# Attention's output projection: all heads in one tile of 128 rows, and three jobs placed later behind POOL

## The chip, the cores and the metric

The kernel runs on one core of a Trainium2 chip. The metric is device time of one execution in microseconds. Before the change it is 6233.53 us, the median of 3 runs (6230.06 to 6236.76).

## The reference, cut to what matters

Two layers run one after the other on `x` of shape (4, 128, 64, 64), float32, that is 4 images of 4096 tokens with 128 channels.

```python
# layer 0: attention over the tokens of one image, 4 heads of 32 channels
Q, K, V = split_heads(x_flat @ Wq + bq), ...
attn = softmax(einsum('bhnd,bhmd->bhnm', Q, K) * scale)
out  = einsum('bhnm,bhmd->bhnd', attn, V)          # heads side by side: 128 channels
y    = out @ Wo + bo + x_flat                      # output projection and residual
y    = layernorm(y) * gamma + beta                 # over the 128 channels of a token
# layer 1: three branches of y, summed
spatial  = conv3x3(y) + bias
spectral = irfft2(W_spec applied to rfft2(y))
ym       = mamba(y)       # in_proj, 4-tap conv, silu, selective scan of 256 x 16 states, gate, out_proj
```

## The kernel before, in words

**Chunks, halves, slots and steps.** The tokens are cut into 32 chunks of 512. A chunk's four heads are handled as two halves `H` (two heads each, `k = H % 2`), and a half meets the image's 4096 keys in 32 tiles of 128. One such tile is a step, and 64 steps, one chunk's two halves, are a slot. The outermost loop counts steps `t` and writes the order of all engines by hand; no scheduler changes it. A slot's number here is that of the chunk whose attention runs in it, and a step's number runs from 0 to 63 within its slot.

**What every step does.** PE computes the scores of one tile for the exponentials (`scores_for_exp`, L480: four matmuls of Q and K and two that subtract the maxima `MX`), the scores for the next half's maxima (`scores_for_max`, L436: four matmuls) and the previous tile's product with the values (`times_values`, L500: two matmuls into `po`). ACT takes the exponentials `e` (L488). DVE reduces the second scores to maxima `part` (L443). Each of these scores has one PSUM buffer, so PE cannot write the next before ACT or DVE has read the last. On even steps DVE also runs one state of layer 1's scan (L817), two slots behind; ACT makes its decay `dA` (L801) and POOL its input term `db` (L806, two states ahead), its product with C (`hs`, L827) and its sum (`acc`, L846).

**Everything else is a job.** A job is a Python generator that `Plan.step` moves on. At each `yield` it names what it needs: a place on PE (`P`), DVE (`D`) or ACT (`A`) and a PSUM bank (`B`, two in all, `m0` and `m1`). During attention an odd step has two places on each engine, an even one has one on ACT. An empty `yield` only waits for the next step. Instructions on POOL and loads on SP's queue need no place. `plan.at(t, rank, job)` starts a job at a step.

**The jobs around the change.** The last step of a half evicts `po`, which has 33 rows for each of two heads, 32 of values and one of the softmax's sum, at rows 0 and 64: ACT copies the first (L509) and DVE the second (L510) into `oz[k]`, one fixed tile for each half of a chunk whose unused rows stay zero. `normalise` then takes the two sum rows through DRAM (`zd`, `zc`), inverts them on DVE (L524), spreads the inverse over the rows by DMA (`rd`, then `rz`, L530) and multiplies on POOL (L533). `output_projection` adds the folded bias `bo` to the residual `xr` on ACT (L548) and, for each of four tiles of 128 tokens, accumulates two matmuls of `oz` with a zero-padded `Wo` (L556) and one of `xr` with the identity (L557) in `py`. `bn_stats` (L564), a reciprocal root on ACT and POOL, and `xh` (L587) follow; `xh` releases layer 1's input jobs: transposes `pt` (L638), input projections (L664), four-tap convolution on DVE (L674, L679), sigmoids in steps on ACT, DVE (L611) and POOL, projections `pd` (L700) and `pdt` (L714). The DT job ends in three POOL multiplies for each half of the 256 channels (`spe`, `dt`, `u`: L739 to L741) and a scaling of `xs` on ACT that waits for them (L748). `maxima` gathers a half's maxima on DVE (`mx`, L449), widens them on POOL (`wide`, L452), transposes them on PE (`pm`, L459) and forms `MX` on ACT and DVE (L466, L467), which the half's first scores need. `scan_output` gates a chunk's scan sums on POOL (L938) and projects them on PE (L948). `convolve` is nine matmuls (L891) and one more. `project_q` (L412) and `project_kv` (L350, L364) make Q, K and V.

**Start and tail.** All constants are loaded by DMAs that ACT issues (L197 to L251) ahead of its first activation, `khi` (L355). After the last half the scan of the last two chunks goes on alone, with its input term on DVE and its sum on PE (L839, L840).

Of the kernel before, what the change touches and what calls it, by code (L numbers as in the profile page):

```python
# [9 lines left out]
F32 = mybir.dt.float32  # L10
F32R = mybir.dt.float32r
AF = mybir.ActivationFunctionType
ALU = mybir.AluOpType
# [4 lines left out]
P = 128  # L18
W = 64
HEADS = 4  # L20
HD = P // HEADS
PAIRS = HEADS // 2
HS = P // 2
L = 512
RPC = L // W
TPC = L // P
# [129 lines left out]
def attention_then_conv_mamba(  # L156
# [17 lines left out]
    nc = tc.nc  # L174
# [3 lines left out]
    NT = N // P  # L178
# [4 lines left out]
    const = ctx.enter_context(tc.tile_pool(name="const", bufs=1))  # L183
    att = ctx.enter_context(tc.tile_pool(name="att", bufs=2))
# [10 lines left out]
    for h in range(HEADS):  # L195
        k, j = divmod(h, 2)
        nc.scalar.dma_start(wk_t[:, h, :], wk[k, :, j * HS : j * HS + HD])  # L197
    wat = const.tile([P, 1 + PAIRS, P], F32, name="wat_vo")
    nc.scalar.dma_start(wat[:, 0, :], wvo[0])
    for h in range(HEADS):  # L200
        k, j = divmod(h, 2)
        c = COL["bk"] + k
# [2 lines left out]
        )  # L205
    Wk = wk_t.rearrange("c h d -> c (h d)")
    Wv = wat[:, 0, :]
    Wo = [wat[:, 1 + k, :] for k in range(PAIRS)]

    wq_t = const.tile([P, PAIRS, 2, 2, HD], F32, name="wq_t")  # L210
    bq = const.tile([P, PAIRS], F32, name="bq")
    for h in range(HEADS):
        k, j = divmod(h, 2)
        c = COL["bq"] + h
# [10 lines left out]
    nc.scalar.dma_start(cst, consts[:, :K_SEL])  # L225
    sel_f = loc.tile([P, P], F32, tag="sg0", name="sel_f", bufs=1)
    nc.scalar.dma_start(sel_f, consts[:, K_SEL:])
    bvk = const.tile([P, PAIRS], F32, name="bvk")
    nc.vector.memset(wat[:, 1:, :], 0.0)
    nc.vector.memset(bvk, 0.0)  # L230
    for h in range(HEADS):
        row = h % 2 * HS
        hs = slice(h * HD, (h + 1) * HD)
        nc.scalar.dma_start(wat[row : row + HD, 1 + h // 2, :], wvo[1, hs, :])
        nc.scalar.dma_start(
            bvk[row : row + HD, h // 2 : h // 2 + 1], bv[0:1, hs].rearrange("o c -> c o")
        )
    vec = const.tile([P, NCOL], F32, name="vec")
    nc.scalar.dma_start(vec, vecs)
    cw = const.tile([P, 9, P], F32, name="cw")  # L240
# [16 lines left out]
    ident = cst[:, K_ID : K_ID + P]  # L257
# [13 lines left out]
    bo = const.tile([P, 1], F32, name="bo")  # L271
# [6 lines left out]
    def constants_of_the_rest():  # L278


        yield ""
        half = loc.tile([P, 2, 2 * P], F32, tag="sg1", name="half", bufs=1)
        nc.vector.tensor_scalar(half, spw, 0.5, None, ALU.mult)
        rr, ir = half[:, 0, :P], half[:, 0, P:]
        ri, ii = half[:, 1, :P], half[:, 1, P:]
        yield ""
        g_id = loc.tile([P, P], F32, tag="ob", name="g_id", bufs=1)
        nc.gpsimd.tensor_tensor(g_id, rr, ii, ALU.add)
        nc.gpsimd.tensor_tensor(cw[:, 4, :], cw[:, 4, :], g_id, ALU.add)
        nc.gpsimd.tensor_tensor(g_flip, rr, ii, ALU.subtract)  # L290
        nc.gpsimd.tensor_tensor(g_hil, ri, ir, ALU.subtract)
        nc.gpsimd.tensor_tensor(g_fliphil, ri, ir, ALU.add)
        yield ""
        nc.vector.tensor_scalar(sbias, cst[:, K_G : K_G + W], col("spec_bi"), None, ALU.mult)
        nc.vector.tensor_tensor(sbias[:, 0:1], sbias[:, 0:1], col("spec_br"), ALU.add)

        nc.scalar.activation(negA, vec[:, COL["A_log"] : COL["A_log"] + NH * NS], AF.Exp)
        yield ""
        nc.vector.tensor_scalar(negA, negA, -1.0, None, ALU.mult)


        bank = yield "PB"
        pb = bank_tile(bank, [P, 1], "pb")
        for k in range(PAIRS):
            nc.tensor.matmul(pb, Wo[k], bvk[:, k : k + 1], start=k == 0, stop=k == PAIRS - 1)
        yield "D"
        plan.release(bank, 2)
        nc.vector.tensor_tensor(bo, pb, col("bo"), ALU.add)
# [5 lines left out]
        [const.tile([P, L], F32R, name=f"K_{k}_{i}") for i in range(NCH)] for k in range(PAIRS)  # L314
    ]
    VA = [const.tile([P, TPC, HEADS, HD + 1], F32, name=f"V_{i}") for i in range(NCH)]

    oz = [const.tile([P, L], F32, name=f"oz{k}") for k in range(PAIRS)]
    for k in range(PAIRS):
        nc.gpsimd.memset(oz[k], 0.0)  # L320
    state = const.tile([P, NH * NS], F32, name="state")
    carry = const.tile([P, NH, TAPS - 1], F32, name="carry")

    rows = [slice(j * HS, (j + 1) * HS) for j in range(2)]
    used = [slice(j * HS, j * HS + HD + 1) for j in range(2)]

    plan = Plan(2, {"x": 2, "f": 1})

    def bank_tile(bank, shape, name):
        return psum.tile(shape, F32, tag=f"m{bank}", name=name)  # L330
# [114 lines left out]
    def maxima(H):  # L445

        bank = yield "B"
        mx = att.tile([P, TPC, 2], F32, tag="mx", name=f"mx_{H}")
        nc.vector.tensor_reduce(mx, part.pop(H), AX.X, ALU.max)  # L449
        wide = att.tile([P, TPC, 2, HS], F32, tag="wide", name=f"wide_{H}", bufs=1)  # L450
        for t in range(TPC):
            nc.gpsimd.tensor_copy(  # L452
                wide[:, t], mx[:, t].unsqueeze(2).to_broadcast([P, 2, HS])
            )
        yield ""
        yield ""
        pm = bank_tile(bank, [P, L], f"pm_{H}")
        for t in range(TPC):
            nc.tensor.transpose(  # L459
                pm[:, t * P : (t + 1) * P], wide[:, t].rearrange("p j d -> p (j d)"), ident  # L460
            )
        yield ""
        plan.release(bank, 2)
        mhi = att.tile([P, L], F32R, tag="th", name=f"mhi_{H}", bufs=1)
        mm = att.tile([P, L], F32R, tag="MX", name=f"MX_{H}")
        nc.scalar.activation(mhi, pm, AF.Copy, scale=-1.0)  # L466
        nc.vector.scalar_tensor_tensor(mm, mhi, minus_lo, pm, ALU.mult, ALU.subtract)  # L467
        MX[H] = mm

    es, po = {}, {}  # L470

    def scores_for_exp(H, m):

# [17 lines left out]
    def times_values(H, m):  # L491

        k = H % PAIRS
        i, t = divmod(m, TPC)
        assert have["V", i] == H // PAIRS // NCH
        if m == 0:
            po[H] = psum.tile([P, L], F32, tag="o", name=f"po_{H}")
        e = es.pop((H, m))
        for j in range(2):
            nc.tensor.matmul(  # L500
                po[H][used[j], :],
                VA[i][:, t, 2 * k + j, :],
                e[:, j, :],
                start=m == 0,
                stop=m == NT - 1,
            )
        if m == NT - 1:
            p = po.pop(H)
            nc.scalar.activation(oz[k][used[0], :], p[used[0], :], AF.Identity)  # L509
            nc.vector.tensor_copy(oz[k][used[1], :], p[used[1], :])  # L510

    def normalise(H, t0):

        k = H % PAIRS
        yield ""
        zd = dram.tile([2, L], F32, tag="zd", name=f"zd_{H}")
        for j in range(2):
            nc.sync.dma_start(zd[j : j + 1, :], oz[k][j * HS + HD : j * HS + HD + 1, :])
        yield ""
        zc = att.tile([P, 2 * L // P], F32, tag="zc", name=f"zc_{H}")  # L520
        nc.sync.dma_start(zc, zd.rearrange("h (a c) -> (h a) c", c=2 * L // P))
        yield ""
        yield ""
        nc.vector.reciprocal(zc, zc)  # L524
        rd = dram.tile([2, L], F32, tag="rd", name=f"rd_{H}")
        nc.sync.dma_start(rd.rearrange("h (a c) -> (h a) c", c=2 * L // P), zc)
        yield ""
        r = att.tile([P, L], F32, tag="r", name=f"rz_{H}", bufs=1)
        for j in range(2):
            nc.sync.dma_start(r[rows[j], :], rd[j : j + 1, :].to_broadcast([HS, L]))  # L530
        yield ""
        yield ""
        nc.gpsimd.tensor_tensor(oz[k], oz[k], r, ALU.mult)  # L533
        if k == PAIRS - 1:
            plan.at(t0, 0, output_projection(H // PAIRS))

    xrs = {}

# [4 lines left out]
    def output_projection(c):  # L543


        xr = xrs.pop(c)
        yield "A"
        nc.scalar.activation(xr, xr, AF.Identity, bias=bo)  # L548
        bank = yield "PB"
        py = bank_tile(bank, [P, TPC, P], f"py_{c}")  # L550
        for t in range(TPC):
            if t == TPC // 2:
                yield "P"
            ts = slice(t * P, (t + 1) * P)
            for k in range(PAIRS):
                nc.tensor.matmul(py[:, t, :], oz[k][:, ts], Wo[k], start=k == 0, stop=False)  # L556
            nc.tensor.matmul(py[:, t, :], xr[:, ts], ident, start=False, stop=True)  # L557


        yield "D"  # L560
# [7 lines left out]
        r = att.tile([P, TPC], F32, tag="rs", name=f"r_{c}")  # L568
# [355 lines left out]
    def scan_output(c):  # L924
# [13 lines left out]
                nc.gpsimd.tensor_tensor(accs[c, hf], accs[c, hf], gates[c][hf], ALU.mult)  # L938
        if not late:
            wr = load_flipped(c)  # L940
        yield ""
        yield ""
        bank = yield "PB"
        pf = bank_tile(bank, [P, L], f"py1_{c}")
        for hf in range(NH):
# [43 lines left out]
    for b in range(B):  # L989


        t0 = (b * NCH - 1) * SLOT + 5
# [7 lines left out]
    for H in range(HALVES):  # L1000
        if H % PAIRS == 0:
            plan.at((H - 1) * NT - LEAD - 24, 0, load_q(H // PAIRS))
        plan.at((H - 1) * NT - LEAD - 14, 0, project_q(H))
        plan.at(H * NT - LEAD, 0, maxima(H))
        plan.at((H + 1) * NT + 1, 0, normalise(H, (H + 1) * NT + 9))
    for c in range(CHUNKS):
        t0 = (c + 1) * SLOT
        plan.at(t0, 0, load_residual(c))
# [127 lines left out]
```

## Time and profile before

| | |
|---|---|
| median of 3 runs | 6233.53 us (6230.06 to 6236.76) |
| the profiled execution | 6236.14 us, of which the program's span is 6234.4 |
| mean granted TensorE clock | 0.982 |
| busy share of the span | PE 96%, POOL 73%, DVE 69%, ACT 58% |
| output projection, L556 and L557 | 768 matmul records, 2 for each matmul |
| transposes of maxima, L459 | 256 records, 1 for each |
| POOL's multiplies L533 | 64, mean 1280 ns |
| idle PE in 2483.62 to 2667.26 us | 0.68 us of 183.64 |
| idle PE in 5063.60 to 5250.66 us | 4.54 us of 187.06 |

The span is that of the one execution that the profiler recorded. Busy shares are averages over the whole span; a stretch has to be read from the timeline, which gives start, duration and, in brackets, how long the engine was idle before and what ended it. A matmul's end is modelled, so the distance between starts tells more than the duration. A float32 matmul leaves two records, a transpose one. Lines that write a tile of the program are named by it, without its number.

### The profile page before, as it was taken

To read this page: it belongs to the slowest core of one execution; us is meant where nothing else is said; L and a number is where in the kernel's file an instruction comes from. 1 tells how busy PE (TensorE), PEld (TensorE's weight loads), DVE (VectorE), ACT (ScalarE), POOL (GpSimd) and SP (SyncE) were. 2 spreads that over 40 slices of the span, in tenths; PEclk is the share of its full clock that TensorE was granted. 3 is DMA by queue.
4 is the path that set the end of the run, shared out by engine and by line. 5 is a ranking of instruction groups with operands and counts; after the bars stand their busy time and mean duration, and the time that the engine had idled before them with its cause. 6 is when DMAs were issued, how large, how long until landed. Compare 5 with 4: busy or idle time off the path is not lost. (4 is left out here: it accounts for less than half of the span.)

```text
span 6234.4 us, 83338 instructions
## 1 busy us (share of the span) xinstructions
PE 6005.2 (96%) x32076; PEld 2540.9 (41%) x32076; DVE 4286.5 (69%) x4406; ACT 3585.0 (58%) x4858; POOL 4579.0 (73%) x4819
## 2 busy tenths in 40 slices
PE   5999999999999999999999999999999999999966
PEld 2444444444444444444444444444444444444321
DVE  4556776777777676777667777776777666767647
ACT  1455666565666555666656566665566556556643
POOL 0005887778887777888787888777788777778877
PEclk7999999999999999999999999999999999999987
DMA  3001222223222222222322221122322211112223
GB/s 111 14 25 47 63 56 61 63 64 98 79 71 60 63 65 60 62 63 73 89 82 65 61 65 60 57 64 67 98 66 71 55 54 54 54 55 58 63 80 85
DMA packets 234624, 404.97 MB, mean 65 GB/s; under 512 B 39272, under 2 KB 40816, under 8 KB 234224
## 3 DMA queue, kind: packets, MB, share of 16 engines
q1 hardware_dynamic: 229840, 397.75, 22.6%
q8 instruction: 251, 4.11, 0.3%
q10 hardware_dynamic: 4384, 1.89, 0.1%
q14 instruction: 149, 1.22, 0.1%
HBM read 350.54 MB, written 49.02 MB: 64 GB/s over the span
## 5 line engine op out<-in xcount | busy, mean ns | idle before, releaser
L443 DVE TENSOR_REDUCE part<-s 128x2 f32<-128x1024 f32 x2048 | 2501.7, 1222 | 1627.4 <-PE s L436 1625.9
L488 ACT ACTIVATE e<-s 128x1024 f32<-128x1024 f32 x2048 | 2095.5, 1023 | 2271.7 <-PE s L480 2263.0
L500 PE MATMUL po<-e,V 128*33 128x512 f32 x8192 | 2160.9, 606 | 2.6 <-DVE oz L510 0.3
L480 PE MATMUL s<-Q,K 64*128 64x512 f32 x8192 | 1504.7, 445 | 22.3 <-ACT e L488 18.5
L436 PE MATMUL s<-K,Q 64*128 64x512 f32 x8192 | 1322.2, 400 | 41.2 <-DVE part L443 39.6
L827 POOL TENSOR_TENSOR hs<-hs,bc 128x512 f32<-128x512 f32 x952 | 1215.5, 1277 | 177.5 <-DVE hs L817 108.6
L480 PEld LDWEIGHTS s<-Q,K 64*128 64x128 f32 x8192 | 610.7, 185 | 1748.9 <-ACT e L488 1179.0
L806 POOL TENSOR_TENSOR db<-u,bc 128x512 f32<-128x512 f32 x948 | 1214.8, 1281 | 0.0
L846 POOL TENSOR_TENSOR acc<-acc,hs 128x512 f32<-128x512 f32 x900 | 1150.9, 1279 | 70.5
L817 DVE TENSOR_TENSOR_SCAN hs<-dA,state,db 128x512 f32<-128x512 f32 x832 | 1060.7, 1275 | 86.0 <-ACT dA L801 54.0
L436 PEld LDWEIGHTS s<-K,Q 64*128 64x128 f32 x8192 | 766.3, 186 | 276.7 <-DVE part L443 99.4
L480 PE MATMUL s<-MX,sel 64*128 64x512 f32 x4096 | 810.9, 392 | 0.0
L826 POOL COPY state<-hs 128x1 f32<-128x1 f32 x864 | 160.2, 185 | 844.8 <-DVE hs L817 844.8
L801 ACT ACTIVATE dA<-dt,negA 128x512 f32<-128x512 f32 x1024 | 702.6, 686 | 116.0 <-DVE hs L817 63.6
L500 PEld LDWEIGHTS po<-e,V 128*33 128x33 f32 x8192 | 299.3, 109 | 913.8 <-issue 879.7
L480 PEld LDWEIGHTS s<-MX,sel 64*128 64x128 f32 x4096 | 384.6, 185 | 92.6
L891 PE MATMUL pf<-xp,cw 128*128 128x512 f32 x576 | 288.2, 617 | 0.0
L452 POOL COPY wide<-mx 128x128 f32<-128x128 f32 x256 | 63.4, 294 | 200.7 <-DVE mx L449 200.7
L817 DVE TENSOR_TENSOR_SCAN hs<-dA,zero,db 128x512 f32<-128x512 f32 x128 | 163.2, 1275 | 7.7 <-POOL db L806 7.4
L840 PE MATMUL acc<-V,cst 128*128 128x512 f32 x128 | 90.1, 807 | 78.2 <-POOL V L827 78.0
L533 POOL TENSOR_TENSOR oz<-oz,rz 128x512 f32<-128x512 f32 x64 | 81.9, 1280 | 107.1 <-DMA rz<-rd 107.1
L891 PEld LDWEIGHTS pf<-xp,cw 128*128 128x128 f32 x576 | 96.2, 188 | 132.4 <-issue 127.4
(144 smaller groups left out, 3847.8 us busy)
## 6 DMA issues: line engine op xcount, KB each, us to landing
bc<-bcd SPq DMA_DIRECT2D x487, 512.0 KB
K<-kd SPq DMA_DIRECT2D x64, 256.0 KB
rz<-rd SPq DMA_DIRECT2D x128, 128.0 KB
K<-bcd SPq DMA_DIRECT2D x42, 256.0 KB
vd<-vst SPq DMA_DIRECT2D x32, 264.0 KB
V<-vd SPq DMA_DIRECT2D x32, 264.0 KB
xq<-in_x SPq DMA_DIRECT2D x32, 256.0 KB
xk<-in_x SPq DMA_DIRECT2D x32, 256.0 KB
```

The lines of the kernel that those rows point to most:

```text
L436: nc.tensor.matmul(sc[:, j, :], QT[H][rows[j], n, t * P : (t + 1) * P], KK[k][m][rows[j], :], start=n == 0, stop=n == 1,)
L443: nc.vector.tensor_reduce(part[H][:, t, :, m], sc, AX.X, ALU.max)
L480: nc.tensor.matmul(s[:, j, :], sel[rows[j], :] if n == 2 else KK[k][i][rows[j], t * P : (t + 1) * P], mov[rows[j], :], start=n == 0, stop= ...
L488: nc.scalar.activation(e, s, AF.Exp)
L500: nc.tensor.matmul(po[H][used[j], :], VA[i][:, t, 2 * k + j, :], e[:, j, :], start=m == 0, stop=m == NT - 1,)
L801: nc.scalar.activation(dA[c, v], dts[c][hf], AF.Exp, scale=negA[:, k : k + 1])
L806: engine.tensor_tensor(db[c, v], us[c][hf], bcs[c, n][0], ALU.mult)
L817: nc.vector.tensor_tensor_scan(hs, dA.pop((c, v)), db.pop((c, v)), state[:, k : k + 1] if c % NCH else zero, ALU.mult, ALU.add,)
L826: nc.gpsimd.tensor_copy(state[:, k : k + 1], hs[:, L - 1 :])
L827: nc.gpsimd.tensor_tensor(hs, hs, bcs[c, n][1], ALU.mult)
L846: nc.gpsimd.tensor_tensor(accs[c, hf], accs[c, hf], hs, ALU.add)
L891: nc.tensor.matmul(pf, cw[:, k, :], xps[c][:, dy : dy + RPC, dx : dx + W], start=k == 0, stop=False)
```

## The change

Four edits are made. The normalised heads of a chunk are gathered in one tile of 128 rows: each half's eviction goes to a buffer `oz` of its own, DMAs copy its two groups of 32 rows into a tile `op`, the inverse sums are spread over 32 rows a head, and POOL multiplies once a chunk, after the second half. The projection is then one matmul of `Wo` with 512 columns, in the channel-by-token layout; DVE adds the bias and the residual in one operation, and four transposes bring the sum to the token layout. Since `Wo` needs no zero rows, it and `bv` are loaded by one DMA each. The projection is placed three steps later, and one step is added ahead of the maxima's transposes and ahead of the scan's output projection.

```diff
-    wat = const.tile([P, 1 + PAIRS, P], F32, name="wat_vo")
+    wat = const.tile([P, 2, P], F32, name="wat_vo")
...
-    Wo = [wat[:, 1 + k, :] for k in range(PAIRS)]
+    Wo = wat[:, 1, :]
...
-    bvk = const.tile([P, PAIRS], F32, name="bvk")
-    nc.vector.memset(wat[:, 1:, :], 0.0)
-    nc.vector.memset(bvk, 0.0)
-    for h in range(HEADS):
-        row = h % 2 * HS
-        hs = slice(h * HD, (h + 1) * HD)
-        nc.scalar.dma_start(wat[row : row + HD, 1 + h // 2, :], wvo[1, hs, :])
-        nc.scalar.dma_start(
-            bvk[row : row + HD, h // 2 : h // 2 + 1], bv[0:1, hs].rearrange("o c -> c o")
-        )
+    bvc = const.tile([P, 1], F32, name="bvc")
+    nc.scalar.dma_start(Wo, wvo[1])
+    nc.scalar.dma_start(bvc, bv.rearrange("o c -> c o"))
...
-        for k in range(PAIRS):
-            nc.tensor.matmul(pb, Wo[k], bvk[:, k : k + 1], start=k == 0, stop=k == PAIRS - 1)
+        nc.tensor.matmul(pb, Wo, bvc, start=True, stop=True)
...
-    oz = [const.tile([P, L], F32, name=f"oz{k}") for k in range(PAIRS)]
-    for k in range(PAIRS):
-        nc.gpsimd.memset(oz[k], 0.0)
...
     def maxima(H):
...
-        yield ""
-        yield ""
+        for _ in range(3):
+            yield ""
         pm = bank_tile(bank, [P, L], f"pm_{H}")
...
     def times_values(H, m):
...
-            nc.scalar.activation(oz[k][used[0], :], p[used[0], :], AF.Identity)
-            nc.vector.tensor_copy(oz[k][used[1], :], p[used[1], :])
+            oz[H] = att.tile([P, L], F32, tag="oz", name=f"oz_{H}", bufs=1)
+            nc.scalar.activation(oz[H][used[0], :], p[used[0], :], AF.Identity)
+            nc.vector.tensor_copy(oz[H][used[1], :], p[used[1], :])
...
     def normalise(H, t0):
-        k = H % PAIRS
-        yield ""
+        c, k = divmod(H, PAIRS)
+        yield ""
+        if k == 0:
+            sums[c] = att.tile([P, L], F32, tag="op", name=f"op_{c}", bufs=1)
+            inverse[c] = att.tile([P, L], F32, tag="r", name=f"rz_{c}", bufs=1)
+        head = [slice((2 * k + j) * HD, (2 * k + j + 1) * HD) for j in range(2)]
+        o = oz.pop(H)
         zd = dram.tile([2, L], F32, tag="zd", name=f"zd_{H}")
         for j in range(2):
-            nc.sync.dma_start(zd[j : j + 1, :], oz[k][j * HS + HD : j * HS + HD + 1, :])
+            nc.sync.dma_start(zd[j : j + 1, :], o[j * HS + HD : j * HS + HD + 1, :])
+        for j in range(2):
+            nc.sync.dma_start(sums[c][head[j], :], o[j * HS : j * HS + HD, :])
...
-        r = att.tile([P, L], F32, tag="r", name=f"rz_{H}", bufs=1)
         for j in range(2):
-            nc.sync.dma_start(r[rows[j], :], rd[j : j + 1, :].to_broadcast([HS, L]))
-        yield ""
-        yield ""
-        nc.gpsimd.tensor_tensor(oz[k], oz[k], r, ALU.mult)
+            nc.sync.dma_start(inverse[c][head[j], :], rd[j : j + 1, :].to_broadcast([HD, L]))
         if k == PAIRS - 1:
-            plan.at(t0, 0, output_projection(H // PAIRS))
+            yield ""
+            yield ""
+            nc.gpsimd.tensor_tensor(sums[c], sums[c], inverse.pop(c), ALU.mult)
+            plan.at(t0, 0, output_projection(c))
...
     def output_projection(c):
         xr = xrs.pop(c)
-        yield "A"
-        nc.scalar.activation(xr, xr, AF.Identity, bias=bo)
+        bank = yield "PB"
+        pa = bank_tile(bank, [P, L], f"pa_{c}")
+        nc.tensor.matmul(pa, Wo, sums.pop(c), start=True, stop=True)
+        yield "D"
+        plan.release(bank, 2)
+        nc.vector.scalar_tensor_tensor(xr, pa, bo, xr, ALU.add, ALU.add)
         bank = yield "PB"
         py = bank_tile(bank, [P, TPC, P], f"py_{c}")
         for t in range(TPC):
-            if t == TPC // 2:
-                yield "P"
-            ts = slice(t * P, (t + 1) * P)
-            for k in range(PAIRS):
-                nc.tensor.matmul(py[:, t, :], oz[k][:, ts], Wo[k], start=k == 0, stop=False)
-            nc.tensor.matmul(py[:, t, :], xr[:, ts], ident, start=False, stop=True)
+            nc.tensor.transpose(py[:, t, :], xr[:, t * P : (t + 1) * P], ident)
...
     def scan_output(c):
...
-        yield ""
-        yield ""
+        for _ in range(3):
+            yield ""
         bank = yield "PB"
...
-        plan.at((H + 1) * NT + 1, 0, normalise(H, (H + 1) * NT + 9))
+        plan.at((H + 1) * NT + 1, 0, normalise(H, (H + 1) * NT + 12))
```

More of the change, by code (lines that the diff above doesn't have):

```diff
@@ L468, in maxima @@
         MX[H] = mm
-    es, po = {}, {}
+    es, po, oz = {}, {}, {}
     def scores_for_exp(H, m):
@@ L508, in times_values @@
             p = po.pop(H)
-            nc.scalar.activation(oz[k][used[0], :], p[used[0], :], AF.Identity)
-            nc.vector.tensor_copy(oz[k][used[1], :], p[used[1], :])
+            oz[H] = att.tile([P, L], F32, tag="oz", name=f"oz_{H}", bufs=1)
+            nc.scalar.activation(oz[H][used[0], :], p[used[0], :], AF.Identity)
+            nc.vector.tensor_copy(oz[H][used[1], :], p[used[1], :])
+    sums, inverse = {}, {}
     def normalise(H, t0):
-        k = H % PAIRS
+        c, k = divmod(H, PAIRS)
         yield ""
+        if k == 0:
[3 more added lines that the diff above has]
+        o = oz.pop(H)
         zd = dram.tile([2, L], F32, tag="zd", name=f"zd_{H}")
         for j in range(2):
-            nc.sync.dma_start(zd[j : j + 1, :], oz[k][j * HS + HD : j * HS + HD + 1, :])
+            nc.sync.dma_start(zd[j : j + 1, :], o[j * HS + HD : j * HS + HD + 1, :])
+        for j in range(2):
+            nc.sync.dma_start(sums[c][head[j], :], o[j * HS : j * HS + HD, :])
         yield ""
```

## The prediction

> **What bounds the kernel now.** First the page's busy times, to find the engine.
>
> ```profile
> PE 6005.2 (96%) x32076; PEld 2540.9 (41%) x32076; DVE 4286.5 (69%) x4406; ACT 3585.0 (58%) x4858; POOL 4579.0 (73%) x4819
> ```
>
> TensorE (PE) at 96% is the candidate, but ends of matmuls are modelled, so starts decide. A step of the kernel begins with the first matmul of L480. The PE timeline around chunk 12's output projection (columns: start, us, instruction, count of records):
>
> ```profile
> 2509.66 0.73 PE L480 MATMUL s<-Q,K 64*128 64x512 f32 x4
> ...
> 2512.14 0.73 PE L480 MATMUL s<-Q,K 64*128 64x512 f32 x4
> 2512.71 0.39 PE L480 MATMUL s<-MX,sel 64*128 64x512 f32 x2
> 2512.94 0.64 PE L436 MATMUL s<-K,Q 64*128 64x512 f32 x4
> 2513.51 0.71 PE L556 MATMUL py<-wat_vo,oz 128*128 128x128 f32 x4
> 2514.06 0.39 PE L557 MATMUL py<-cst,xr 128*128 128x128 f32 x2
> ...
> 2516.38 1.05 PE L500 MATMUL po<-e,V 128*33 128x512 f32 x4
> 2517.37 0.73 PE L480 MATMUL s<-Q,K 64*128 64x512 f32 x4
> ```
>
> Every instruction follows on the last with no idle bracket. A bare step takes 2.34 to 2.36 us (2604.84 to 2607.19); the one with the projection takes 2517.37 - 2512.14 = 5.23. Other steps in the same timeline: one 128x512 job 3.41 (2607.19 to 2610.59), two 4.27 (2624.51 to 2628.78), four transposes `pt` 2.94 (2540.79 to 2543.73). So PE instructions are the clock of the attention part, and a removed one is saved, unless another engine is late in that step.
>
> Second, where others are late. Two slots (64 steps, one chunk), one early and one in the last batch, in the stretches view (length; then busy PE, PEld, DVE, ACT, POOL):
>
> ```profile
> 2483.62:2667.26 183.64, 182.96 (x995) 78.49 (x994) 131.48 (x135) 111.25 (x152) 145.08 (x156) 0.99 0.23 61
> 5063.60:5250.66 187.06, 182.52 (x990) 76.17 (x988) 131.15 (x135) 111.44 (x151) 147.15 (x157) 1.00 0.20 55
> ```
>
> The later slot has no K/V projection to do (1.06 + 1.09 us of jobs), yet is 3.4 us longer: some 5.6 us of stalls. The timelines of POOL, ACT, PE and DVE there show the chain:
>
> ```profile
> 5079.56 1.28 POOL L741 TENSOR_TENSOR u<-dt,xs 128x512 f32<-128x512 f32 x1
> ```
> ```profile
> 5080.87 0.72 ACT L748 ACTIVATE xs<-xs,vec 128x512 f32<-128x512 f32 x1 [1.19 <-POOL u L741]
> ```
> ```profile
> 5082.55 0.73 PE L480 MATMUL s<-Q,K 64*128 64x512 f32 x4 [1.40 <-ACT e L488]
> ```
> ```profile
> 5084.93 1.28 DVE L817 TENSOR_TENSOR_SCAN hs<-dA,zero,db 128x512 f32<-128x512 f32 x1 [3.49 <-POOL db L806]
> ```
>
> Two chains of three POOL multiplies (`spe`, `dt`, `u`: 6 x 1.28 = 7.7 us) stand back to back; ACT and DVE stall behind them, then PE. In the early slots the chains stand six steps apart and PE loses almost nothing by them.
>
> **What the Trainium skill says.** "TensorE: Matmul & The Clock Gate", Step-by-step, has a stream cost its moving columns, each instruction's drain hidden by the next: the trace agrees in kind (records 112 ns apart for 128 columns, some 430 for 512), but each f32 matmul here has two records, so the page's one-pass 55.6 and 215.7 ns are not used. "Perfetto Trace Analysis", Optimizing Tensor Performance, prefers a true transpose to a matmul; here four transposes add 0.59 us and twelve 128-column matmuls 2.88. "PSUM — Partial Sum Buffer", Engine vs sequencer instructions, says that ScalarE, VectorE and GpSimdE take their queues strictly in order: the 3.49 us above is that. "DMA: Bandwidth & Descriptors", Issuing engines are not separate DMA queues, says that an issue occupies the issuing sequencer only; on ACT here that is 0.472 us each.
>
> **The change part by part.** Places come from the two kernels' instruction lists set side by side, prices from the trace.
>
> (a) *Projection.* Out: 8 matmuls on `oz` and 4 on `xr`, 5.23 - 2.35 = 2.88 us a chunk. In: one 128x512 matmul, listed in the step of a Q projection, so at the second job's price 4.27 - 3.41 = 0.86; and four transposes, 0.59. Saving 1.43; 31 chunks: **-44 us**. ACT loses a 0.71 us activation a chunk and DVE gains a 0.74 us one; neither paces PE by itself.
>
> (b) *Maxima's transposes, one step later.* Now in half of the cases PE starts with POOL still writing:
>
> ```profile
> 2557.53 1.00 POOL L452 COPY wide<-mx 128x128 f32<-128x128 f32 x4
> ```
> ```profile
> 2557.91 0.99 PE L459 MATMUL pm<-cst,wide 128*128 128x128 f32 x4
> ```
>
> That step took 3.28, 0.93 over bare (the copies' pace); the other one of the slot, beside two jobs, adds 0.39. Both become 0.59: -0.14 a slot, **-4 us**. The scan's output (L948) waits 3.1 us in two places for POOL: **-3 us** with its extra step.
>
> (c) *POOL and SP.* 32 of 64 multiplies L533 go (32 x 1.28 = 41 us), POOL being no pace-setter: 0. SP issues 128 new copies `op<-oz` at about 0.5 us; its queue mostly waits and the `rz` copies halve. They stand before the `zc` load, so a half's normalisation may come 1 us later; it has until the projection, listed two steps (4.7 us) later than now: 0. Reuse of `oz`, `op` and `r` is 20 or more steps away: 0. If that cover went, PE would stand behind POOL's multiply by the excess.
>
> (d) *What moves with it.* `xh` comes six steps later and every job behind it, so the packing of all slots changes. Relief: after the half's eviction PE now waits for a reduction (step of 3.10 against 2.35); the list puts a DT projection and a convolution in the step ahead: -0.75. A step of 2.67 by the maxima's DVE work gets the transposes: -0.32. New: `bn_stats` with a sigmoid's DVE operation in a step without a matmul job; that is the pattern of the late slot at 5106.98, where PE waits 0.8 us. Three double steps of two convolution taps each, without jobs: DVE needs 2 x 1.2 + 1.25 + 2 x 0.66 = 5.0 us against 4.7, three times, less about 0.5 of slack: 0.5. POOL's two chains now four steps apart (six before) with the multiply between: after them 4.1 + 4.1 + 1.3 + 3.9 = 13.3 us of POOL work against 13.8 of PE time (2.34 + 2.48 + 2.34 + 2.35 + 4.27 for the five steps), on a backlog of one chain, so that `db` is about 1 us late: 0.8 with what follows. Sum +1.0, less 0.5 of such waits that the early slots have already, -1.07: about -0.5 to 0.5 a slot; 31 slots: **0, bounds -35 and +45**.
>
> (e) *The last batch.* Its slots get the same spaced chains as all others, so the 5.6 us go, up to 6 x 5.6 = 34. I take half to two thirds, for the new packing has its own waits: **-19 us**.
>
> (f) *Start.* ACT issues all constants' loads before its first activation:
>
> ```profile
> 17.99 0.43 ACTq L235 DMA_DIRECT2D bvk<-in_bv  x1
> ...
> 21.98 1.27 ACT L355 ACTIVATE khi<-pk,bk 128x512 fp32r<-128x512 f32 x2 [19.97 <-DMA dtw<-in_dt_w]
> ```
>
> Eight issues become two: 6 x 0.472 = 2.8, on the path as PE waits for `khi`'s successors. **-3 us** (0 if a DMA comes last).
>
> (g) *Tail.* After 5987 the scan of the last two chunks runs, with the last projection in it. PE waits 18.3 us for `oz` there and DVE 6.3 for `py`. The projection now starts three steps later and its result four; DVE has scan work to fill two of these waits, but more of the input chain falls behind. No row decides: **+3, bounds -7 and +12**.
>
> Sum: -44 - 4 - 3 + 0 - 19 - 3 + 3 = -70, on the profiled execution's 6236.1 us (span 6234.4). The median of the runs, 6233.5, lies 2.6 lower, and the same -70 from it gives **6164 us**.
>
> **The rivals.** *Exchange only (0.25).* Packing gives as much as it takes and the last batch keeps its stalls in other steps: -44 - 3 - 3 and little else, 6184. For it: waits that vanish at one step often show at another. Against it: the stalls have one named cause, which the list undoes. *POOL becomes the bound (0.06, slower).* If the multiply pushes the second chain so far that each of 24 earlier slots stalls as the late slot does now, 3.2 us at the three steps behind the chains (3.83, 3.09 and 3.28 against 2.35), it costs 24 x 3.2 = 77 against a gain of 50: 6260. It decides when POOL's state multiply starts over 10 us after its step's begin; it did 9.1 in the early slots and 12.6 in the late. The 13.3 against 13.8 above speaks against it. *The exponentials pace the step (0.04, no change).* If ACT's `e` (1.02 us) and the scores in one PSUM buffer were the loop, PE work removed would come back as waiting: 6231. Against it: a bare step is 2.35 us, and in it ACT is idle over 1.3 us before `e`.
>
> **How the numbers follow.** The forecast's own case (0.65) gives 6164. Its bounds (d, e, g) give 6125 to 6208; the range 6128 to 6210 takes in the first rival and leaves out the last two. A run of this kernel cannot tell less than 0.2%, 12 us, from no change. Faster by more: 0.90; within: 0.04; slower: 0.06.
>
> **What would show it.** Right: per chunk one `pa` of 128x512 and a four-record transpose group, slots of about 182 us early and 181 to 184 in the last batch, `pm` steps near 2.94, khi's start near 19.2. Wrong: PE idle before L436 or L480 growing by over 1.5 us a slot with POOL's `db` or `u` as the releaser; `pa` waiting for `op`; a tail over 260 us.

## The result, and the profile after

The changed kernel takes 6149.28 us (median of 4 runs, 6147.69 to 6149.89), beside 6235.15 us for the kernel before in the same comparison. The ratio is 0.9863, with a 95% interval from 0.9851 to 0.9875. The forecast was 6164 us, with 6128 to 6210 as its range; the gain is 86 us where 70 were expected.

The profiled execution's span fell from 6234.4 to 6147.9 us. The busy times of the page of after (engine, us, share of the span, instructions):

```profile
PE 5943.8 (97%) x31498; PEld 2470.2 (40%) x31498; DVE 4324.6 (70%) x4436; ACT 3573.6 (58%) x4826; POOL 4542.8 (74%) x4785
```

PE is still the bound, with 61 us less of busy time. Slots 12 and 27 in the stretches view of after (the prediction showed slots 13 and 27 of before; slot 12 took 183.55 us there):

```profile
2271.67:2454.92 183.25, 181.66 (x983) 75.85 (x981) 133.50 (x136) 111.53 (x151) 145.61 (x157) 1.00 0.22 61
5009.36:5189.49 180.13, 179.71 (x973) 74.63 (x971) 131.66 (x135) 110.09 (x149) 145.85 (x157) 1.00 0.22 57
```

The late slot was the longer one and is now the shorter one: 187.06 us have become 180.13, and its idle PE 0.42 us. The early slot still has 1.6 us of idle PE and is hardly shorter than before; that will matter below. The new projection, in the PE timeline of after at step 13 (start, us, instruction, records):

```profile
2307.55 0.73 PE L468 MATMUL s<-Q,K 64*128 64x512 f32 x4
...
2308.92 1.13 PE L400 MATMUL pq<-xq,wq_t 128*128 128x512 f32 x2
2309.89 1.02 PE L547 MATMUL pa<-op,wat_vo 128*128 128x512 f32 x2
...
2311.82 0.73 PE L468 MATMUL s<-Q,K 64*128 64x512 f32 x4
```

There is no idle bracket: `pa` stands behind the Q projection `pq`, POOL's multiply is long done, and the step is 4.27 us, two jobs. Lines of after: scores for the exponentials L468, scores for the maxima L424, `pa` L547, POOL's multiply L532.

Where the 86.5 us of the span come from, measured from starts of steps in both traces; the forecast column spreads the prediction's terms a to c over the slots that have a projection:

| stretch | before, us | after, us | difference | forecast |
|---|---|---|---|---|
| span's start to first step | 131.4 | 127.9 | -3.5 | -3 |
| slots 0 to 2 | 507.8 | 504.3 | -3.5 | -3.3 |
| slot 3 | 188.6 | 180.1 | -8.5 | -1.6 |
| slots 4 to 24 | 3863.9 | 3835.0 | -28.9 | -34.5 |
| slots 25 to 30 (last batch) | 1120.3 | 1085.9 | -34.4 | -28.9 |
| slot 31, to its last step | 171.6 | 168.0 | -3.6 | -1.6 |
| from the last step to the end | 250.9 | 246.7 | -4.2 | +3 |

### The profile page after: what moved, and what is told of

Its sections match the earlier page's. It is cut to its first block, busy times and chain, and to the rows that moved or that the text cites. A ratio compares the mean times of both kernels' runs of the same rounds, so it can differ in the third digit from the quotient of the medians.

```text
span 6147.9 us, 82348 instructions
## 1 busy us (share of the span) xinstructions
PE 5943.8 (97%) x31498; PEld 2470.2 (40%) x31498; DVE 4324.6 (70%) x4436; ACT 3573.6 (58%) x4826; POOL 4542.8 (74%) x4785
## 5 line engine op out<-in xcount | busy, mean ns | idle before, releaser
L468 PE MATMUL s<-Q,K 64*128 64x512 f32 x8192 | 1503.5, 445 | 8.8 <-ACT e L476 2.9
L424 PE MATMUL s<-K,Q 64*128 64x512 f32 x8192 | 1322.7, 400 | 39.8 <-DVE part L431 38.5
L468 PEld LDWEIGHTS s<-Q,K 64*128 64x128 f32 x8192 | 610.9, 185 | 1730.3 <-ACT e L476 1178.4
L424 PEld LDWEIGHTS s<-K,Q 64*128 64x128 f32 x8192 | 762.5, 186 | 271.7 <-DVE part L431 93.3
L468 PE MATMUL s<-MX,sel 64*128 64x512 f32 x4096 | 812.8, 393 | 1.3 <-DVE MX L455 1.1
L468 PEld LDWEIGHTS s<-MX,sel 64*128 64x128 f32 x4096 | 383.9, 184 | 99.5 <-DVE MX L455 9.1
L837 PE MATMUL acc<-V,cst 128*128 128x512 f32 x128 | 89.5, 799 | 72.8 <-POOL V L824 72.6
L686 POOL TENSOR_TENSOR xs<-xs,sg_x 128x512 f32<-128x512 f32 x64 | 82.8, 1295 | 69.2 <-ACT sg_x L610 69.2
```

The source lines that it names most:

```text
L424: nc.tensor.matmul(sc[:, j, :], QT[H][rows[j], n, t * P : (t + 1) * P], KK[k][m][rows[j], :], start=n == 0, stop=n == 1,)
L468: nc.tensor.matmul(s[:, j, :], sel[rows[j], :] if n == 2 else KK[k][i][rows[j], t * P : (t + 1) * P], mov[rows[j], :], start=n == 0, stop= ...
```

## The experiments

Each time stands beside the after's 6149.28 and before's 6232 to 6235 us, the medians of before in the same comparisons. Steps and slots are numbered as above.

**Only the matmul.** The changed kernel with the later placements taken back:

```diff
-        for _ in range(3):
-            yield ""
+        yield ""
+        yield ""
         pm = bank_tile(bank, [P, L], f"pm_{H}")
...   (the same two lines ahead of pf in scan_output)
-        plan.at((H + 1) * NT + 1, 0, normalise(H, (H + 1) * NT + 12))
+        plan.at((H + 1) * NT + 1, 0, normalise(H, (H + 1) * NT + 9))
```

> The changed kernel with all three later placements taken back: two empty steps ahead of the maxima's transposes and of the scan's output as before, the projection due at step 9 instead of 12. The single long matmul stays. Theory 1 (the placement behind POOL is needed): POOL's multiply of the gathered heads ends 2.2 us into step 10 in the changed kernel, but the matmul now stands in step 9 on PE, so PE waits up to 3.2 us a slot, 31 x 3.2 = 99 us, and the last batch keeps its two chains back to back (about 185.6 us a slot there): 6250 to 6290 us. Theory 2 (the shorter projection is all there is, the placements are worth little): 6235 - 44 - 3 = 6188 us, with early slots near 182.2 and no PE idle before the projection's matmul.

Measured: 6403.41 us, ratio to before 1.0275 (1.0260 to 1.0290), slower. The PE timeline of this kernel at step 9, and POOL's at the same place:

```profile
2373.33 0.64 PE L424 MATMUL s<-K,Q 64*128 64x512 f32 x4
2378.12 2.07 PE L547 MATMUL pa<-op,wat_vo 128*128 128x512 f32 x2 [4.16 <-POOL op L532]
2380.13 1.92 PE L488 MATMUL po<-e,V 128*33 128x512 f32 x4
2381.98 1.22 PE L468 MATMUL s<-Q,K 64*128 64x512 f32 x4
```
```profile
2376.81 1.26 POOL L532 TENSOR_TENSOR op<-op,rz 128x512 f32<-128x512 f32 x1
```

PE waits 4.16 us for `op`, and then its matmuls run at half speed: the two records of `pa` start 1.01 us apart instead of 0.43, and `po` takes 1.92 us instead of 1.05. The stretches view gives the granted clock, third from the end, there and right behind:

```profile
2376.54:2383.36 6.82, 5.24 (x12) 1.85 (x14) 0.00 (x0) 0.00 (x0) 6.64 (x7) 0.50 0.18 45
2383.40:2386.00 2.60, 2.60 (x20) 1.19 (x16) 1.93 (x2) 1.59 (x3) 2.50 (x2) 1.00 0.00 0
```

Step 9 lasts 9.46 us where one job makes 3.41. So Theory 1 holds in kind, but the total lies 113 us above its range, for its price of 3.2 us a slot was half of the 6.05 measured: the multiply came 1.0 us later than in the changed kernel, and the slow restart at half clock, 1.9 us in this step and 0.5 in the next (2.96 instead of 2.47), was not thought of. The transposes of the maxima wait again as well, 21.9 us in all for `wide` against 0.7 in the changed kernel. The matmul without its place is a loss of 171 us.

**Only the place.** The kernel before with three steps instead of two at both places and the projection due at step 12, keeping its twelve short matmuls:

```diff
-        yield ""
-        yield ""
+        for _ in range(3):
+            yield ""
         pm = bank_tile(bank, [P, L], f"pm_{H}")
...   (the same ahead of pf in scan_output)
-        plan.at((H + 1) * NT + 1, 0, normalise(H, (H + 1) * NT + 9))
+        plan.at((H + 1) * NT + 1, 0, normalise(H, (H + 1) * NT + 12))
```

> The kernel before with only the three later placements: three empty steps instead of two ahead of the maxima's transposes and of the scan's output, the projection due at step 12 instead of 9. The old twelve short matmuls stay. Theory 1 (the gain of the last batch comes from the list's order, not from PE's instructions): slots 25 to 30 fall from 187.05 to about 181.0 + 1.4 = 182.5 us, 27 us in all, early slots move by less than 0.7 us each, total 6195 to 6210 us. Theory 2 (it comes with the shorter projection): slots 25 to 30 stay at 186 to 187 us and the total within 6 us of 6235.

Measured: 6185.87 us, ratio 0.9926 (0.9911 to 0.9941). Slots 25 to 30 fall to 181.3 to 182.0 us, slot 3 from 188.6 to 180.4, the early slots stay (3858.9 us for slots 4 to 24 against 3863.9). Theory 1 holds, and the total came below its range mostly because slot 3, which it did not count, gained 8.2 us. More than half of the change's gain, 46 us, needs no shorter projection at all. Which of the three later places does it was not tried apart.

**Empty places.** The kernel before, with jobs of no instruction in the last batch:

```diff
+    def hold(b, i):
+        for _ in range(3):
+            yield ""
+        bank = yield "PB"
+        yield "DA"
+        plan.release(bank, 2)
+        yield ""
+        bank = yield "PB"
+        yield "A"
+        plan.release(bank)
...
+    for i in range(NCH):
+        plan.at((B - 1) * NCH * SLOT + i * SLOT + 40, 0, hold(B, i))
```

> The kernel before with one addition: in the last batch, jobs without any instruction take the places and PSUM banks that the K and V projections of a next batch would have taken, so that all other jobs of slots 25 to 30 fall where they fall in the early slots. Theory 1 (the 5.6 us of stalls of a late slot are those of the two POOL chains standing back to back): slots 25 to 30 go to 183.6 - 2.15 = 181.4 us, 6 x 5.6 = 34 us less, total about 6201 us. Theory 2 (the late slots are slow for another reason, for instance their loads): slots 25 to 30 stay at 187 us, total 6235 us.

Measured: 6197.35 us (6191.07 to 6203.52), ratio 0.9947 (0.9931 to 0.9964). The late slot in the stretches view of this kernel:

```profile
5050.86:5232.32 181.46, 180.83 (x990) 76.90 (x988) 130.66 (x134) 110.23 (x150) 147.22 (x157) 1.00 0.23 56
```

With the same 990 PE instructions as before the change, slot 27 takes 181.46 instead of 187.06 us: the 5.6 us were the order of the list and nothing else. Slots 25 to 30 together fall from 1120.3 to 1090.8 us. Slot 3, which has no such held place, stays at 188.6. In slot 3 of the kernel before, DVE works on both halves' `dt` in one step (step 2), as in the last batch, and the two POOL chains follow back to back: it was a seventh slot of that kind.

**The projection due one step earlier.** The changed kernel with the projection due at step 11 (`+ 12` becomes `+ 11`).

> The changed kernel with one number altered: the projection is due at step 11 instead of 12, so its matmul stands alone in step 11, the reductions for the norm stand in step 17 instead of in step 19 beside a sigmoid's DVE operation. Theory 1 (PE's 0.88 us of waiting in step 21 of each slot comes from these two DVE operations in one step): step 21 goes from 3.23 to 2.35 us, 31 x 0.88 = 27 us less, about 6122 us. Theory 2 (the wait only moves to another step): 6145 to 6152 us. Theory 3 (the matmul now waits for POOL's multiply, which ends 2.2 us into step 10): step 11 longer than 3.41 us, total above 6155 us.

Measured: 6145.03 us (6144.23 to 6149.04), ratio 0.9861 (0.9847 to 0.9876). Theory 2: step 21 does fall to 2.35 us, but step 19 now takes 2.87, and steps 33 and 34 together 0.9 us more than a bare pair, so the wait moved. Step 11 is 3.40 us, one job, so `pa` doesn't wait: two steps earlier than in the changed kernel POOL's multiply is still in time. On PE its order differs from that of "only the place" in the steps of the projection alone. There steps 11, 13, 15 and 17 take 2.35 + 4.75 + 3.89 + 2.35 = 13.34 us, here 3.40 + 3.42 + 2.93 + 2.35 = 12.10: the short form saves 1.24 us a chunk with `pa` as a step's only job, and the two kernels lie 40.8 us apart.

**The matmul twice.**

```diff
-        nc.tensor.matmul(pa, Wo, sums.pop(c), start=True, stop=True)
+        for _ in range(2):
+            nc.tensor.matmul(pa, Wo, sums[c], start=True, stop=True)
+        sums.pop(c)
```

> The changed kernel with the projection's 128x512 matmul issued twice into the same bank, once a chunk. It stands behind a Q projection in step 13. Theory 1 (PE's instructions are the clock of the attention part, a second job of a step costs 0.86 us): step 13 goes from 4.27 to 5.13 us, slots from 182.1 to 183.0, 32 x 0.86 = 27.5 us more, about 6177 us. Theory 2 (another engine paces the slot, so PE work is hidden in part): 6149 to 6160 us.

Measured: 6171.41 us (6168.21 to 6172.39), ratio 0.9899 (0.9882 to 0.9915). Step 13 goes from 4.27 to 5.13 us, the 0.86 expected; the sum is 22 us and not 27.5. Slots 4 to 24 took the full price (17.8 us, 0.85 each); in the last batch step 21, the one that waits, was shorter (3.46 to 3.23 on average), and slots 3 and 31 and the tail did not grow. PE's instructions are the clock.

**A multiply for each half.** The changed kernel with POOL's multiply done on 64 rows after each half:

```diff
-        if k == PAIRS - 1:
-            yield ""
-            yield ""
-            nc.gpsimd.tensor_tensor(sums[c], sums[c], inverse.pop(c), ALU.mult)
+        yield ""
+        yield ""
+        own = slice(2 * k * HD, 2 * (k + 1) * HD)
+        nc.gpsimd.tensor_tensor(sums[c][own, :], sums[c][own, :], inverse[c][own, :], ALU.mult)
+        if k == PAIRS - 1:
             plan.at(t0, 0, output_projection(c))
```

> The changed kernel with POOL's normalising multiply done for each half on its own 64 rows, as before the change, that is 64 multiplies of 512 columns instead of 32, 32 x 1.28 = 41 us more on POOL. Theory 1 (POOL has the room, a saved multiply was worth nothing): within 6 us of 6149, the busy time of POOL up by 41 us. Theory 2 (POOL's queue is at its limit and part of the gain came from the 32 multiplies saved): up to 41 us more, 6190 us.

Measured: 6142.70 us (6141.28 to 6144.47), ratio 0.9854 (0.9840 to 0.9869), 6.6 us below the changed kernel, with POOL's busy time up by 40 us (4583.2). The 32 multiplies saved were worth nothing, as Theory 1 has it. That more POOL work should come out ahead was in neither theory; step 21 fell from 3.19 to 2.84 us on average, and what shortens it is found below.

**Longer chains.** One, then two more POOL multiplies behind each chain of `spe`, `dt`, `u` (here two; `e` is dead by then):

```diff
         nc.gpsimd.tensor_tensor(u, z, xss[c][hf], ALU.mult)
+        for _ in range(2):
+            nc.gpsimd.tensor_tensor(e, e, e, ALU.mult)
```

> The changed kernel with one more POOL multiply of 128x512, on a tile that is dead by then, behind each of the two chains of a chunk (64 more, 82 us on POOL). POOL's state multiply starts up to 10.4 us after its step in the changed kernel, with PE not waiting, and 12.6 us in the late slots before, with PE waiting 3.2 us at three steps. Theory 1 (a limit lies between these two): the largest lag goes to 11.7 to 13 us and PE begins to wait, 0 to 3.2 us a slot: 6150 to 6250 us, likeliest 6180. Theory 2 (POOL's sum of work decides, and it has 26% to spare): 6149 us with no new wait.

> The changed kernel with two more POOL multiplies of 128x512, on a tile that is dead by then, behind each of the two chains of a chunk (128 more, 164 us on POOL, its busy share up to about 76%). Theory 1 (the length of the backlog behind a chain decides, not the sum): the largest lag of POOL's state multiply goes past 13 us, PE waits at the steps behind the chains for over 3.2 us a slot, above 6250 us. Theory 2 (the sum decides): 6149 to 6155 us.

Measured: 6204.13 us (ratio 0.9953, 0.9938 to 0.9968) with one, 6310.01 us (1.0122, 1.0107 to 1.0138) with two. POOL is 74% busy in both; an added multiply took 1.05 us and not the 1.28 of the others. The scan in the DVE timeline of the kernel with one more, the PE matmul behind it, and the same scan with a multiply for each half:

```profile
2334.35 1.28 DVE L816 TENSOR_TENSOR_SCAN hs<-dA,state,db 128x512 f32<-128x512 f32 x1 [2.16 <-POOL db L805]
```
```profile
2336.80 0.73 PE L424 MATMUL s<-K,Q 64*128 64x512 f32 x4 [1.64 <-DVE part L431]
```
```profile
2313.95 1.28 DVE L815 TENSOR_TENSOR_SCAN hs<-dA,state,db 128x512 f32<-128x512 f32 x1 [0.42 <-POOL db L804]
```

The scan waits for POOL, the reduction `part` that stands behind it in DVE's list is late, and PE waits for that at step 16. Here is step 16 against the largest lag in slot 12, which is how long after the start of its step POOL begins a state's multiply by C (`hs`):

| kernel | largest lag, us | step 16, us |
|---|---|---|
| the changed one | 10.4 | 2.35 |
| a multiply for each half | 10.7 | 2.51 |
| one more in each chain | 12.4 | 4.25 |
| two more in each chain | 14.7 | 6.72 |

Below some 10.5 us of lag nothing is lost; above it each microsecond of lag costs about one (the last row holds a slow restart as well, since PE waits 3.63 us there). The slots of the changed kernel itself agree: step 16 takes 2.36 us at a lag of 9.4 (slot 10), 2.52 at 10.7 (slot 11), 2.96 at 11.1 (slot 25) and 3.32 at 11.5 (slot 3). The length of the backlog decides and not POOL's sum; most slots of the changed kernel stand within a few tenths of the edge, and two are past it.

**Without DVE's small operation.** What is PE waiting for in step 21? PE's wait there in the changed kernel, the DVE timeline ahead of it, and POOL's:

```profile
2331.53 0.73 PE L424 MATMUL s<-K,Q 64*128 64x512 f32 x4 [1.20 <-DVE part L431]
```
```profile
2328.09 0.36 DVE L563 BATCH_NORM_AGGREGATE mv<-st 128x2 f32<-128x6 f32 x4
2328.48 1.27 DVE L567 TENSOR_SCALAR v<-mv 128x4 f32<-128x4 f32 x1
2329.67 0.67 DVE L608 SCALAR_TENSOR_TENSOR sg_z<-zg,ln_z 128x512 f32<-128x512 f32 x1
2330.27 1.21 DVE L431 TENSOR_REDUCE part<-s 128x2 f32<-128x1024 f32 x1
```
```profile
2328.45 1.28 POOL L841 TENSOR_TENSOR acc<-xs,hs 128x512 f32<-128x512 f32 x1
```

An operation on four columns, `v`, takes 1.27 us. It starts 0.03 us after a POOL multiply and ends with it. In the kernel with a multiply for each half the neighbours fall otherwise, and it is short (DVE timeline of that kernel):

```profile
2327.61 0.17 DVE L568 TENSOR_SCALAR v<-mv 128x4 f32<-128x4 f32 x1
```

The Trainium skill's page "SBUF — State Buffer", Who interferes with whom, says that a `tensor_scalar` of DVE in a two-port mode and an instruction of GpSimd take the same pair of SBUF ports, and that the one that comes second is blocked until the first is done. The trace agrees: over slots 4 to 23 of the changed kernel `v` took 0.17 us in ten slots and 0.70 to 1.29 us in the other ten; each long one began during a POOL multiply and ended 0.03 us behind it, and step 21 lasted 2.54 us more than `v` in every slot (2.71 with 0.17, 3.81 with 1.27). That `v` ran in a two-port mode no run shows by itself. With a multiply for each half, `v` was short in 16 of these 20 slots. The edit takes `v` off DVE:

```diff
+    eps = const.tile([P, 1], F32, name="eps")
+    nc.vector.memset(eps, LN_EPS)
     zero = const.tile([P, 1], F32, name="zero")
...
-        nc.vector.tensor_scalar(v, mv[:, :, 1], LN_EPS, None, ALU.add)
...
-        nc.scalar.activation(q, v, AF.Ln)
+        nc.scalar.activation(q, mv[:, :, 1], AF.Ln, bias=eps)
...
+        nc.gpsimd.tensor_scalar(v, mv[:, :, 1], 1.0, LN_EPS, ALU.mult, ALU.add)
         nc.gpsimd.tensor_tensor(q, r, r, ALU.mult)
```

> The changed kernel without DVE's small operation v (128x4, the variance plus epsilon): ACT adds the epsilon as the bias of its logarithm, and POOL forms v for its own use. In the changed kernel v takes 0.17 us in some slots and 1.27 us in others, where it ends with the POOL multiply that started just before it, and slots with the long v last 183.3 us against 182.1. Theory 1 (DVE is held by POOL's running instruction, and PE waits for the reduction behind it): the slots all come to about 181.9 us, 21 x 0.7 + 6 x 0.9 = 20 us less, about 6129 us. Theory 2 (the long v is only how a wait for something else is recorded, or POOL's extra small operation costs as much): 6143 to 6150 us.

> The kernel with the projection due at step 11 and, as in the run before, without DVE's small operation v, which takes 0.93 us there in most slots and stands one step ahead of the step of 2.87 us. Theory 1: that step goes to 2.35 us, 27 x 0.5 = 14 us less than 6145, about 6131 us. Theory 2 (the wait moves to the next reduction): 6140 to 6146 us.

Measured: 6106.76 us (6105.36 to 6108.45), ratio 0.9794 (0.9780 to 0.9807), and 6109.93 us (ratio 0.9799, 0.9785 to 0.9812) with the projection due at step 11. Both are faster than the changed kernel. Theory 1 holds at its step: step 21 went from 3.19 us on average to 2.51, and step 19 of the second from 2.87 to 2.33. But 42 us is twice the 20 expected, and the second gained 35 where 14 were expected. Of the 1.45 us saved in an early slot, 0.68 are step 21; the rest, 0.77, is spread over all steps, 0.01 to 0.03 us in most. Between starts of PE's records in bare steps, those without a job on PE, the largest piece is the first matmul pair of the maxima's scores: 228 instead of 234 ns (means over slots 4 to 23).

**An unused tile.** Is it the new tile `eps`, of four bytes a partition, which may move the tiles behind it in SBUF? The changed kernel with the two lines of `eps` and nothing else:

> The changed kernel with one tile more, eps of 128x1, placed ahead of the tile zero, written once at the start and used by nothing; v stays on DVE. In the kernel without v, which needed this tile, not only step 21 was shorter, by 0.68 us on average, but every step by 0.012 to 0.03 us, 0.77 us a slot in all, most of it between the two matmuls of the maxima's scores. Theory 1 (these 0.77 us come from the later tiles' places in SBUF, moved by the new tile): a bare step falls from 2.355 to 2.343 us and the total to about 6149 - 31 x 0.77 = 6125 us, while step 21 keeps its mean of 3.19 us or so. Theory 2 (they come from v's absence): bare steps stay at 2.355 us and the total at 6144 to 6150 us.

Measured: 6119.27 us (6116.98 to 6119.97), ratio 0.9814 (0.9800 to 0.9827), 30 us below the changed kernel. A bare step fell from 2.354 to 2.340 us, and the same pair of records to 228 ns. So the 0.77 us a slot, 24 us or 0.4%, came with the tile and not with `v`'s absence. That it works by where tiles lie in SBUF, as Theory 1 says, is the likely reading, but no trace shows where they lie. The effect is no chance of one run: bare steps take 2.338 to 2.340 us in the three kernels with the tile and 2.352 to 2.355 in the other eleven. The kernels before (2.353) and after (2.354) are both among these, so no part of the change's own gain is of this kind. Step 21 also fell, from 3.19 to 2.87 on average, for `v` met POOL's multiplies otherwise; that is why it is 30 us and not 24. The further 12.5 us to 6106.76 are what taking `v` off DVE gave.

**Eight loads.** The weights and the bias by four DMAs each:

```diff
-    nc.scalar.dma_start(Wo, wvo[1])
-    nc.scalar.dma_start(bvc, bv.rearrange("o c -> c o"))
+    for h in range(HEADS):
+        hs = slice(h * HD, (h + 1) * HD)
+        nc.scalar.dma_start(Wo[hs, :], wvo[1, hs, :])
+        nc.scalar.dma_start(bvc[hs, :], bv[0:1, hs].rearrange("o c -> c o"))
```

> The changed kernel with the projection's weights and the V bias loaded by eight DMAs again, four of 32 rows and four of 32 values, all issued by ACT. Theory 1 (an issue on ACT stands ahead of the first activation, 0.472 us each): khi starts 6 x 0.472 = 2.8 us later than in the changed kernel, and the first step of attention with it. Theory 2 (a DMA that comes last decides): khi's start and the first step move by less than 0.5 us.

The ACT timelines of this kernel and of the changed one:

```profile
21.96 0.69 ACT L345 ACTIVATE khi<-pk,bk 128x512 fp32r<-128x512 f32 x1 [19.95 <-DMA dtw<-in_dt_w]
```
```profile
19.65 1.26 ACT L343 ACTIVATE khi<-pk,bk 128x512 fp32r<-128x512 f32 x2 [17.63 <-DMA dtw<-in_dt_w]
```

`khi` starts 2.3 us later and the first step 3.5 us later (131.4 us). The one run took 6147.8 us, though, so no loss at the end is shown: step 21 happened to be shorter in it (2.94 instead of 3.19 us over slots 4 to 24, 5 us in all), which covers the later start. Over all profiled executions, `khi` starts at 21.7 to 22.0 us in the four kernels with eight loads and at 19.1 to 19.8 in the ten with two; the first step follows at 130.2 to 131.4 and at 126.9 to 128.8, but for one of the ten (the kernel of 6109.93 us: 131.0). The issues set `khi`, and in all but that one the first step follows.

## Why the prediction was right, point by point

**(a) Projection, -44: right in size and in kind.** "The matmul twice" gives the 0.86 us of a second job, and the pair of kernels that differ on PE in the projection alone gives 1.24 us a chunk with the matmul as a first job (1.05), so 1.43 with it as a second.

**(b) Transposes, -4, and the scan's output, -3: right.** The two `pm` steps carry 0.59 us each (0.93 and 0.39 before), and PE's waits for POOL's `acc` ahead of the scan's output, 3.1 us in all before, are gone.

**(c) POOL and SP at nothing: right.** 32 multiplies put back cost nothing.

**(d) What moves with it, at 0: within its bounds, but in part by luck.** The early slots gave 28.9 us where (a) to (c) make 34.5, so the new order cost 5.6, or 0.27 a slot. The prediction's own parts do not make 0: 0.8 + 0.5 + 0.8 - 0.75 - 0.32 - 0.5 is +0.5 a slot, the upper end of what it gave; its +1.0 already has the relief of 1.07 in it, and the lower end takes that off again. Of the named parts, step 2 gave 0.74 (0.75 said) and step 30 0.32 (as said). The wait behind `bn_stats` was put in the right place and at the right size, 0.85 against 0.8, for half a reason: the sum of DVE work explains 0.17 of it, and the other 0.68 is `v` held by POOL. The three steps of convolution taps cost nothing (0.5 said), and POOL's chains 0.02 (0.8 said). Measured, these parts make a gain of 0.19 us a slot; the other 0.46 up to the cost of 0.27 lies in steps that were not taken apart. Two terms put too high stood against costs that nobody named.

**(e) The last batch, -19: the mechanism right, the term too small.** The 5.6 us are exact for slot 27 ("empty places": 187.06 to 181.46), and over slots 25 to 30 that experiment gave 29.5 us. Of these the change kept -34.4 + 6 x 1.65 = -24.5. So the new order did have waits of its own, some 5 us, and step 21 alone lost more than that there (3.46 us against 2.35); the caution was right in kind and 5.5 us too large. And the count of six was wrong. Slot 3 has the same two chains back to back, which its length (188.6 beside 183.6) tells; it gave 8.5 us where 1.6 were counted.

**(f) Start, -3: right.** `khi` came 2.3 us earlier and the first step 3.5. The price of 0.472 us an issue holds: in this one execution ACT's later issues began 0.5 us late, and seven of the ten kernels with two loads have `khi` at 19.1 to 19.2, as predicted, 2.8 us earlier. That this reaches the end is not shown by a time.

**(g) Tail, +3: wrong in sign.** It gave -4.2, inside its bounds of -7 and +12. There PE's one wait for `op` is 21.3 us, where it was 18.3 for `oz` before, the 3 us said. The wait of 4.1 us ahead of that one, for ACT's `xs`, is gone, but one of 5.2 us for DVE's `xr` is new; PE's waits for POOL's products `V` fell from 78.0 to 72.6 us. Together these are -1.3 us; the rest of the tail was not taken apart.

The gains missed are 6.9 us (slot 3), 5.5 (last batch), 7.2 (tail), 2.0 (slot 31) and 0.7 (ahead of slot 3), less 5.6 lost in the early slots: 16.7 us, within rounding the distance of -86.5 from -70. The sum came near because the two large terms, (a) and (e), were right or too cautious, and because errors cancelled in (d).

**The rivals.** "Exchange only" would have kept the last batch's stalls; they went with the order alone. "Exponentials pace the step" falls with the matmul issued twice. "POOL becomes the bound" did not come, but its place was judged well and its chance perhaps too low: it was to decide from a lag of 10 us, the edge is at some 10.5, and the changed kernel runs at 10.4.

## What to carry to other kernels

Where one engine's queue is the clock, a change's price is that of its instructions and of the order it forces on every job behind it; run the two apart, for here the shorter matmul alone lost 171 us and the order alone won 46. Tabulate the length of every period of a loop before the change, since slots that stand out by a few microseconds show how often a stall occurs. And before a difference of half a per cent is laid to an edit, run the edit's memory layout alone.

## What the runs showed of the hardware

- A PE wait of 4.16 us was followed by 5.2 us of matmuls at half the granted clock, 2.4 us lost on top of the wait. The Trainium skill's page "TensorE: Matmul & The Clock Gate", What's actually happening, says that the array's clock is halved after an idle window of about 3.4 us and comes back after a busy one as long; the trace agrees in kind, with a granted clock of 0.50 for 6.8 us in all, though the clock fell 2.6 us after the modelled end of the last matmul and not 3.4. The wait of 3.63 us at step 16 with two more POOL multiplies shows it too (a clock of 0.50 from 1.1 us after PE's restart, for 3.4 us, and scores of 1.22 and 1.05 us instead of 0.73 and 0.64); the wait of 1.64 us with one more doesn't (clock 1.00).
- A DVE `tensor_scalar` of 128x4 lasted 0.17 to 1.29 us, by whether a POOL multiply had begun just before it.
- An unused tile of four bytes a partition, placed ahead of others, shortened a pair of PE's score matmuls from 234 to 228 ns, a bare step from 2.354 to 2.340 us and the kernel by 0.4%. Whether it is an operand's place in SBUF, whose, and which places are good, was not tried.
